# A two-layer transformer on one core: in the first feed-forward, half of the row transposes go from the matrix engine to VectorE and DMA, and the order of the weight chunks changes

## The chip, the cores and the metric

The kernel runs on one core of one Trainium2 chip. The metric is the device time of one execution in microseconds (us); runs are compared by their medians. The engines are called by the names that the profile uses: PE is the matrix engine (PEld its weight loads), DVE is VectorE, ACT is ScalarE, POOL is GpSimd, SP is the engine that issues most DMAs.

## The reference, cut to what matters

The input is x with 2 sequences of 512 rows of 512 floats. Four blocks follow one another, each with a residual and a layernorm: a linear attention over a fixed memory, a feed-forward with ternary weights, a softmax attention, and an ordinary gated feed-forward. The change touches the second block and the end of the first:

```python
def _L0_ffn_ref(x, w_gate, w_up, w_down):
    xf = x.astype(jnp.float32) / 128.0
    gate = jnp.einsum('bsh,ih->bsi', xf, w_gate)
    up = jnp.einsum('bsh,ih->bsi', xf, w_up)
    inter = jax.nn.silu(gate) * up
    inter_q = jnp.trunc(jnp.clip(inter * 128.0, -128.0, 127.0)).astype(jnp.int8)
    down = jnp.einsum('bsi,hi->bsh', inter_q.astype(jnp.float32), w_down)
    out = jnp.trunc(jnp.clip(down * 128.0, -128.0, 127.0)).astype(jnp.int8)
    return out
...
x = _layernorm(x + _L0_attn_ref(x, ...), axis=-1)
x = _layernorm(x + _L0_ffn_ref(x, w_gate, w_up, w_down), axis=-1)
```

The intermediate size is 1376, which the kernel cuts into 11 chunks: ten of 128 and a last one of 96.

## The kernel before, in words

Rows lie 128 to a tile, so each sequence has four row tiles `xs[b][0..3]`. A matmul needs the rows transposed, with the 512 features on the partitions in four blocks of 128.

**The end of the first attention.** `read` (L392) takes one row tile: eight PE products, one per head (L401), four heads at a time. For each head ACT reads the denominator (L405); DVE takes the reciprocals (L409); ACT scales the first three heads (L414) and POOL adds them (L418, L427), and DVE adds the other five to the row (L423). The loop at L516 reads the eight row tiles in order, and inside tile i it normalizes tile i-1: `norm_a0` (L495) takes the statistics on DVE, the reciprocal root on POOL (L143, L144), the offset on DVE (L503), and writes the normalized row on ACT (L504).

**The transposed rows of the first feed-forward.** `split(b)` (L254) makes them for one sequence. For each block k, PE transposes the four row tiles into one PSUM bank (L264), ACT copies the bank to SBUF rounded to the short format [...] (`his`, L265), and DVE keeps the rest (`los`, L266). Sequence 0 is turned in the loop at L516, while the tiles 5 and 6 are read; sequence 1 is turned in the feed-forward, between its third and fourth chunk (L678 to L681).

**The chunks.** `up(b, c)` (L560) multiplies chunk c of the gate weights, then of the up weights, with the rows of sequence b: 16 matmuls of 128x512 into two PSUM banks (L567). There are eight banks in all, so PE can be about four chunks ahead of those who empty them. A chunk is finished by a chain that changes engine at nearly each step:

- ACT: silu of the gate, `sg` (L583)
- DVE: times the up half, `y` (L586), then cut to 12 bits (L155)
- ACT: two relus that round toward zero, `ta` and `tb` (L165, L166)
- DVE: their difference is the integer row, `it` (L593)

The weights themselves are divided by their scale on ACT (`divided`, L506, done in L433), into tiles `tu` of which four fit (`query_tile`, L278); chunks 0 to 2 are divided in the loop at L516 by the text, chunks 3 to 10 in the feed-forward, a half after each chunk (L597). `largest` (L172) reads the first tile of the down weights on DVE (L177); PE, DVE and POOL make of it the scale (L184, L195, L199) and the 11 divided tiles `td` (L435), which DVE compares with the originals (`check_down`, L204).

**What sets the order.** Each engine runs its own list in order. For PE, ACT, DVE and SP a scheduler makes the lists at build time from the program's text, the dependences and the `issue_after` ties; POOL keeps the order of the text. So where a helper is called in the text is not always where its instructions stand. In the built program of before, the divisions of chunks 0 to 3 stand on ACT ahead of the eight reads. By chunk the text has (0,0) to (0,2), the transposes of sequence 1, (0,3), (1,0) to (1,2), then the two sequences by turns, (0,4), (1,3), (0,5), (1,4) and so on. The down products follow at L617 and L710 to L725. SP issues the eleven loads of the down weights (L248) when the attention's buffers are free.

Of the kernel before, what the change touches and what calls it, by code (L numbers as in the profile page):

```python
# [10 lines left out]
F32 = mybir.dt.float32  # L11
F32R = mybir.dt.float32r
I32, I16, I8 = mybir.dt.int32, mybir.dt.int16, mybir.dt.int8
PE = mybir.EngineType.PE
AF = mybir.ActivationFunctionType
ALU = mybir.AluOpType
# [3 lines left out]
P = 128  # L20
B, S, HID = 2, 512, 512
NT = S // P
NK = HID // P
NH, G, D = 8, 4, 128
INTER = 1376
CHUNKS = [(i, min(P, INTER - i)) for i in range(0, INTER, P)]
GROUPS = [4, 4, 3]
LN_EPS = 1e-5
DEN_EPS = 1e-6
LAST = HID - 1  # L30
LENT = 3
TOP12 = -4096
BELOW_HALF = 0.5 - 2.0**-13
# [3 lines left out]
def kernel(  # L37
# [19 lines left out]
    nc = tc.nc  # L57
# [6 lines left out]
    xtp = ctx.enter_context(tc.tile_pool(name="xtp", bufs=2))  # L64
# [14 lines left out]
    def psum(name):  # L79
        return ps.tile([P, 512], F32, tag="mm", name=name)  # L80
# [99 lines left out]
    def over_partitions(mx, name):  # L180

        k = mx.shape[-1]
        pm = psum(f"pmx_{name}")
        nc.tensor.transpose(pm[:k, :P], mx, ident)  # L184
        top = small.tile([k, 1], F32, tag=f"top{k}", name=f"top_{name}", bufs=1)
        nc.vector.reduce_max(top, pm[:k, :P], AX.X)
        dg = small.tile([k, k], F32, tag=f"dg{k}", name=f"dg_{name}", bufs=1)
        nc.vector.tensor_scalar_mul(dg, ident[:k, :k], top)
        return dg

    def scales(dg, name):

        k = dg.shape[-1]
        pb = psum(f"pbc_{name}")
        nc.tensor.matmul(pb[:, :k], ones[:k, :], dg, start=True, stop=True)  # L195
        sc = const.tile([P, k], F32, tag=f"sc_{name}", name=f"sc_{name}")
        nc.vector.tensor_scalar(sc, pb[:, :k], 1e-30, 3e38, ALU.max, ALU.min)
        inv = const.tile([P, k], F32, tag=f"inv_{name}", name=f"inv_{name}")
        nc.vector.reciprocal(inv, sc)  # L199
        return sc, inv  # L200
# [50 lines left out]
            wds.append(wd)  # L251
        return wds

    def split(b):  # L254

        hi = xtp.tile([P, NK, S], F32, tag="xt", name=f"xh_{b}").bitcast(F32R)
        los = [pair_tile(f"xl_{b}_{i}").bitcast(F32R) for i in range(2)]
        his = [hi[:, k, :] for k in range(NK)]
        los = [los[k // 2][:, k % 2, :] for k in range(NK)]

        def block(k):
            pt = psum(f"pt_f0{b}_{k}")
            for t in range(NT):
                nc.tensor.transpose(pt[:, ts(t, P)], xs[b][t][:, ts(k, P)], ident)  # L264
            nc.scalar.copy(his[k], pt)  # L265
            nc.vector.tensor_sub(los[k], pt, his[k].bitcast(F32))  # L266

        return his + los, block


    wop = ctx.enter_context(tc.tile_pool(name="wop", bufs=6))
# [6 lines left out]
    def query_tile(name):  # L278
        return wqp.tile([P, 2, HID], F32, tag="wq", name=name)

    with tc.tile_pool(name="a0w", bufs=1) as a0w, tc.tile_pool(name="a0", bufs=2) as a0:
# [213 lines left out]
        def norm_a0(i, steps):  # L495

            b, t = order[i]
            with tc.issue_after(steps[1].ins):
                stats = layernorm_stats(xs[b][t], f"a0{b}_{t}")
            with tc.issue_after(steps[-1].ins):  # L500
                mv, rstd = stats
                off = small.tile([P, 1], F32, tag="off", name=f"off_{i}")
                nc.vector.tensor_scalar(off, mv[:, 0:1], rstd, -1.0, ALU.mult, ALU.mult)  # L503
            nc.scalar.activation(xs[b][t], xs[b][t], AF.Identity, bias=off, scale=rstd)  # L504

        def divided(c, a):  # L506
            n = CHUNKS[c][1]
            if c not in ts_up:
                t = query_tile(f"tu_{c}").bitcast(F32R)
                ts_up[c] = t.rearrange("p a (k i) -> p a k i", k=NK)  # L510
                if n < P:
                    nc.gpsimd.memset(ts_up[c][:, :, :, n:].bitcast(F32), 0.0)
            ternary(nc.scalar, ts_up[c][:, a, :, :n], gus[c][:, a], inv_up[:, a : a + 1])

        ts_up, x2 = {}, []
        for i, (b, t) in enumerate(order):  # L516
            steps = read(b, t, lambda steps: norm_a0(i - 1, steps) if i else None)
            for _ in range((3, 2, 2, 0, 0, 0, 0, 0)[i]):
                check_up(*checks.pop(0))
            if i == 3:  # L520
                tot_up = total(counts, "up")
            elif i == 4:
                flag_up, eff_up = verdict(tot_up, sc_up, "up")
            if i in (3, 4, 5):
                for a in range(2):
                    divided(i - 3, a)
            if i == 5:
                parts, block = split(0)
                x2.append(parts)
            if i in (5, 6):  # L530
                for k in range(2):
                    block(2 * (i - 5) + k)
        norm_a0(len(order) - 1, steps)


    fp = ctx.enter_context(tc.tile_pool(name="fp", bufs=2))

    def inter_tiles(name, dtype=F32):
# [6 lines left out]
            for b in range(B)  # L545
        ]

    wdp = ctx.enter_context(tc.tile_pool(name="wdp", bufs=1))
    wds = down_weights(wd0_in, "0")
    with tc.tile_pool(name="f0", bufs=2) as f0:  # L550
# [9 lines left out]
        def up(b, c, behind=()):  # L560
            n = CHUNKS[c][1]
            t = ts_up[c]
            pp = [psum(f"pg_f0{b}_{c}"), psum(f"pu_f0{b}_{c}")]
            with tc.If(ternary_up > 0) as way:
                for a in range(2):
                    for i in range(2 * NK):
                        nc.tensor.matmul(  # L567
                            pp[a], t[:, a, i % NK, :], x2[b][i],
                            start=(i == 0), stop=(i == 2 * NK - 1),
                        )  # L570
            with way.Else():
                for a in range(2):
                    for i in range(2 * NK):
                        nc.tensor.matmul(
                            pp[a][:n], gus[c][:, a, i % NK, :],
                            x2[b][i].bitcast(F32),
                            start=(i == 0), stop=(i == 2 * NK - 1),
                        )
            sg = fp.tile([P, S], F32, tag="sg", name=f"sg_f0{b}_{c}")
            with ExitStack() as tied:  # L580
                for step in behind:
                    tied.enter_context(tc.issue_after(step.ins))
                nc.scalar.activation(sg[:n], pp[0][:n], AF.Silu, scale=silu_scale[:n])  # L583
            y = f0.tile([P, S], F32, tag="y", name=f"y_f0{b}_{c}")

            step = nc.vector.scalar_tensor_tensor(  # L586
                y[:n], sg[:n], eff_up[:n, 1:2], pp[1][:n], ALU.mult, ALU.mult
            )
            cut_to_12(y[:n])
            ta, tb = truncated_parts(f0, y[:n], n, f"f0{b}_{c}")  # L590

            it = its[b][c // 4][:, c % 4]
            nc.vector.scalar_tensor_tensor(  # L593
                it[:n], tb[:n], 128.0, ta[:n], ALU.min, ALU.subtract
            )
            inter[b].append(it)
            if to_divide:  # L597
                part = to_divide.pop(0)
                if part:
                    divided(*part)  # L600
            return step

        to_divide = [(c, a) for c in range(3, len(CHUNKS)) for a in range(2)]

        counts_d = const.tile([P, len(CHUNKS)], F32, tag="counts_d", name="counts_d")
        nc.gpsimd.memset(counts_d, 0.0)
# [25 lines left out]
            return pd  # L632


        pds, ys, stats, moved = {}, {}, {}, {}

        def scaled(i):
            y = f0.tile([P, HID], F32, tag="y", name=f"yd_{i}")
            moved[i] = nc.scalar.activation(y, pds[i], AF.Copy, scale=down_scale)
            cut_to_12(y)  # L640
            ys[i] = y

# [29 lines left out]
            with tc.issue_after(taken[n if t == NT - 1 else f"f0_{n}"].ins):  # L672
                layernorm_apply(xs[b][t], xs[b][t], stats[i])

        to_divide[2:2] = [None, None]
        for c in range(3):
            up(0, c)
        parts, block = split(1)  # L678
        x2.append(parts)
        for k in range(NK):  # L680
            block(k)  # L681
        step = up(0, 3)
        with tc.issue_after(step.ins):
            mx_d = largest([wds[0]], "down")
        for c in range(3):
            up(1, c)
        top_d = over_partitions(mx_d, "down")
        for c in range(4, 8):
            up(0, c)
            if c == 4:  # L690
                sc_d, inv_d = scales(top_d, "down")
            up(1, c - 1)
            for i in range(2 * c - 8, 2 * c - 6):
                check_down(i)
        up(0, 8)
        up(1, 7)
        check_down(8)
        check_down(9)
        up(0, 9)
        check_down(10)  # L700
        up(0, 10)
        tot_d = total(counts_d, "down")
        up(1, 8)
        flag_d, eff_d = verdict(tot_d, sc_d, "down")
        down_scale = const.tile([P, 1], F32, tag="down_scale", name="down_scale")
        nc.vector.tensor_scalar(down_scale, eff_d, -128.0, None, ALU.mult)
        up(1, 9)
        ternary_d = branch(flag_d)
        for i in range(2):
            f0_down(i)  # L710

        up(1, 10, moved.values())
        for i in range(2, len(order) - 2):
            f0_down(i)

# [565 lines left out]
```

## Time and profile before

| What | us |
|---|---|
| median of the runs (lowest, highest; 3 runs) | 472.47 (472.12, 472.58) |
| the profiled execution: its own time | 471.99 |
| the profiled execution: its span, first to last instruction | 470.0 |
| last read of the attention: PE's last product issued | 130.2 |
| first chunk of the feed-forward: PE's first matmul | 130.65 |
| transposes of sequence 1 on PE | 141.99 to 147.58 |
| end of the first feed-forward on PE | 234.1 |

The times in the last four lines count from the span's start. The chain of waits is followed back from the last instruction: each line has start, length, engine and operation. The timeline has start, length, engine, line, operation, output and inputs, and in square brackets how long the engine had been idle and who ended that. The matmuls of PE are pipelined: a record of 128x512 lasts 0.39 us, and the next one starts 0.23 us after it did.

### The profile page before, as it was taken

To read this page: it belongs to the slowest core of one execution; us is meant where nothing else is said; L and a number is where in the kernel's file an instruction comes from. 1 tells how busy PE (TensorE), PEld (TensorE's weight loads), DVE (VectorE), ACT (ScalarE), POOL (GpSimd) and SP (SyncE) were. 2 spreads that over 40 slices of the span, in tenths; PEclk is the share of its full clock that TensorE was granted. 3 is DMA by queue.
4 is the path that set the end of the run, shared out by engine and by line. 5 is a ranking of instruction groups with operands and counts; after the bars stand their busy time and mean duration, and the time that the engine had idled before them with its cause. 6 is when DMAs were issued, how large, how long until landed. Compare 5 with 4: busy or idle time off the path is not lost.

```text
span 470.0 us, 5725 instructions
## 1 busy us (share of the span) xinstructions
PE 463.0 (99%) x1899; PEld 330.7 (70%) x1899; DVE 327.9 (70%) x622; ACT 268.1 (57%) x507; POOL 114.4 (24%) x141
## 2 busy tenths in 40 slices
PE   9999999999999999999999999999999999999995
PEld 8454444434478788888866568888888888888885
DVE  1265677767857677755988989986666767998633
ACT  3344799557556877645756743575644768532201
POOL 0343101566460090400348032000000000041101
PEclk9999999999999999999999999999999999999998
DMA  8999800000015000213192000000000000001011
GB/s 311 373 348 382 301 2 0 0 0 3 1 54 188 3 1 1 92 47 81 58 360 94 0 1 1 1 0 1 1 0 1 0 1 1 1 24 45 22 46 45
DMA packets 15187, 33.97 MB, mean 72 GB/s; under 512 B 3440, under 2 KB 4336, under 8 KB 15152
## 3 DMA queue, kind: packets, MB, share of 16 engines
q1 hardware_dynamic: 14864, 33.14, 19.6%
q8 instruction: 22, 0.36, 0.3%
q10 hardware_dynamic: 288, 0.36, 0.2%
q14 instruction: 13, 0.11, 0.1%
HBM read 31.40 MB, written 2.10 MB: 71 GB/s over the span
## 4 chain that ended last, share of the span: by engine, by line
PE 72%; ACT 7%; DVE 5%; issue 3%; POOL 0%; POOLq 0%; DVEq 0%; ACTq 0%
PE pm L1071 17%; PE pg_f L567 9%; PE pu_f L567 8%; PE pc L1071 8%; PE pdm L1159 7%; PE pd_f L622 4%; PE pdc L1159 4%; DVE x L423 4%; PE pqk L853 3%; PE po L401 2%; ACT y L414 2%; ACT t L433 2%; PE pv L866 2%; PE pot L949 1%; PE po L965 1%
## 5 line engine op out<-in xcount | busy, mean ns | idle before, releaser
L401 PE MATMUL po<-mw,q 128*128 128x512 f32 x128 | 57.1, 598 | 0.3 <-DVE mv_a L137 0.2
L325 PE MATMUL pq<-xt_a,wq 128*128 128x512 f32 (+1 forms) x152 | 56.9, 526 | 0.0
L143 POOL TENSOR_TENSOR rstd_f<-mv_f,ln_eps 128x1 f32<-128x1 f32 x15 | 4.4, 295 | 172.1 <-DVE mv_f L1174 130.2
L401 PEld LDWEIGHTS po<-mw,q 128*128 128x128 f32 x128 | 23.0, 189 | 32.1 <-issue 17.7
L325 PEld LDWEIGHTS pq<-xt_a,wq 128*128 128x128 f32 x152 | 26.2, 190 | 27.3 <-issue 26.2
L1071 PE MATMUL pm<-r,ugu 128*128 128x512 f32 x152 | 37.7, 389 | 0.0
L1071 PE MATMUL pm<-r,it_early 128*128 128x512 f32 x144 | 36.7, 392 | 0.0
L1071 PEld LDWEIGHTS pm<-r,ugu 128*128 128x128 f32 x152 | 28.5, 188 | 5.9
L1071 PEld LDWEIGHTS pm<-r,it_early 128*128 128x128 f32 x144 | 27.0, 188 | 6.0 <-issue 0.5
L423 DVE SCALAR_TENSOR_TENSOR x<-po,den,x 128x511 f32<-128x511 f32 x40 | 29.8, 745 | 1.9
L165 ACT ACTIVATE ta_f<-y_f,below_half 128x512 int8<-128x512 f32 (+1 forms) x22 | 15.9, 723 | 23.7 <-DVE y_f L155 23.3
L1081 DVE SCALAR_TENSOR_TENSOR ev_q<-pm,ev_q 128x512 f32<-128x512 f32 x27 | 18.6, 687 | 14.1 <-PE pm L1071 14.1
L418 POOL TENSOR_TENSOR y<-y,y 128x511 f32<-128x511 f32 x16 | 20.3, 1272 | 31.5 <-ACT y L414 30.8
L593 DVE SCALAR_TENSOR_TENSOR it_f<-tb_f,ta_f 128x512 fp32r<-128x512 int16 (+1 forms) x22 | 15.2, 690 | 16.3 <-ACT tb_f L166 16.3
L361 ACT ACTIVATE e<-pq,bq 128x512 f32<-128x512 f32 x16 | 11.1, 691 | 24.1 <-PE pq L325 21.7
L567 PE MATMUL pg_f<-xh,tu 128*128 128x512 f32 x88 | 24.7, 401 | 0.0
L1080 ACT ACTIVATE ev_q<-pc 128x512 f32<-128x512 f32 x27 | 16.0, 594 | 14.1 <-PE pc L1071 14.0
L435 POOL TENSOR_SCALAR td<-wd,inv_down 128x512 fp32r<-128x512 f32 x11 | 18.6, 1710 | 22.0 <-DVE inv_down L199 22.0
L567 PE MATMUL pg_f<-xl,tu 128*128 128x512 f32 x88 | 23.6, 390 | 0.0
L567 PE MATMUL pu_f<-xh,tu 128*128 128x512 f32 x88 | 23.6, 389 | 0.0
L567 PE MATMUL pu_f<-xl,tu 128*128 128x512 f32 x88 | 23.5, 389 | 0.0
L961 ACT ACTIVATE x<-x,off_f,rstd_f 128x512 f32<-128x512 f32 x7 | 5.7, 816 | 27.7 <-POOL off_f L960 27.7
(310 smaller groups left out, 1088.3 us busy)
## 6 DMA issues: line engine op xcount, KB each, us to landing
gu<-in_gu SPq DMA_DIRECT2D x20, 512.0 KB, 8.0
wo<-in_wo SPq DMA_DIRECT2D x16, 512.0 KB, 5.7
wd<-in_wd SPq DMA_DIRECT2D x20, 256.0 KB, 4.9
wq<-in_wq SPq DMA_DIRECT2D x8, 256.0 KB, 4.1
x<-in_x SPq DMA_DIRECT2D x7, 256.0 KB, 4.4
out<-x SPq DMA_DIRECT2D x7, 256.0 KB, 2.0
wqkv<-in_wqkv SPq DMA_DIRECT2D x1, 768.0 KB, 10.7
m<-in_m SPq DMA_DIRECT2D x1, 512.0 KB, 5.8
```

The source lines that it names most:

```text
L165: nc.scalar.activation(a[:n], y, AF.Relu, bias=below_half[:n])
L325: done = nc.tensor.matmul(pq[:, at], wq[h][:, k, :], xt[:, k, at], start=(k == 0), stop=(k == NK - 1),)
L401: nc.tensor.matmul(po, qs[b][h0 + j][:, ts(t, P)], mw[:, h0 + j, :], start=True, stop=True,)
L418: nc.gpsimd.tensor_add(ys[0][:, :LAST], ys[0][:, :LAST], y[:, :LAST])
L423: steps.append(nc.vector.scalar_tensor_tensor(x[:, :LAST], four[j][:, :LAST], d, x[:, :LAST], ALU.mult, ALU.add))
L435: eng.tensor_scalar(out, w, factor, None, ALU.mult)
L567: nc.tensor.matmul(pp[a], t[:, a, i % NK, :], x2[b][i], start=(i == 0), stop=(i == 2 * NK - 1),)
L622: nc.tensor.matmul(pd, inter[b][c][:, ts(t, P)], td[c].bitcast(F32R), start=(c == 0), stop=(c == last),)
L1071: nc.tensor.matmul(p, w, x, start=(left[id(p)] == begun[id(p)]), stop=(left[id(p)] == 1))
L1080: nc.scalar.activation(ev, pc, AF.Copy, scale=CROSS)
L1081: nc.vector.scalar_tensor_tensor(ev, pm, MAIN, ev, ALU.mult, ALU.add)
L1159: nc.tensor.matmul(p[:, :w], got[j // 4][1][kind][:, j % 4], down_parts[j][kind][:, cols], start=(j == 0 and kind == kinds[0]), stop=(j == ...
```

## The change

Sequence 0 is still transposed on PE. For sequence 1, DVE transposes each normalized row tile in squares of 32x32 into a tile `squares` (one instruction of 128x512 per row tile), and then 16 DMAs on SP put the squares where a full transpose has them: each moves 32 partitions by 16 runs of 32 floats. `block` reads the result from SBUF.

```diff
+SQ = 32
+LEAD = 6
...
-    def split(b):
+    def split(b, xt=None):
...
         def block(k):
-            pt = psum(f"pt_f0{b}_{k}")
-            for t in range(NT):
-                nc.tensor.transpose(pt[:, ts(t, P)], xs[b][t][:, ts(k, P)], ident)
-            nc.scalar.copy(his[k], pt)
-            nc.vector.tensor_sub(los[k], pt, his[k].bitcast(F32))
+            h, l = his[k], los[k]
+            if xt is None:
+                rows = psum(f"pt_f0{b}_{k}")
+                for t in range(NT):
+                    nc.tensor.transpose(rows[:, ts(t, P)], xs[b][t][:, ts(k, P)], ident)
+            else:
+                rows = xt[:, :, k, :]
+                h, l = (u.rearrange("p (t q) -> p t q", t=NT) for u in (h, l))
+            return (
+                nc.scalar.copy(h, rows),
+                nc.vector.tensor_sub(l, rows, h.bitcast(F32)),
+            )
...
+    def move_squares(squares, xt):
+        src = squares.rearrange("p t (k i) -> p (t k) i", k=NK)
+        dst = xt.rearrange("p t k i -> p (t k) i")
+        for i in range(P // SQ):
+            for j in range(P // SQ):
+                nc.sync.dma_start(dst[ts(j, SQ), :, ts(i, SQ)], src[ts(i, SQ), :, ts(j, SQ)])
...
-                t = query_tile(f"tu_{c}").bitcast(F32R)
+                t = (pair_tile if c in PAIRED else query_tile)(f"tu_{c}").bitcast(F32R)
...
+        PAIRED = (LEAD - 2, LEAD - 1, len(CHUNKS) - 1)
+        def turn_squares(i):
+            b, t = order[i]
+            nc.vector.transpose(squares[:, t, :], xs[b][t])
...
-            if i in (3, 4, 5):
+            if i >= len(order) - LEAD:
                 for a in range(2):
-                    divided(i - 3, a)
+                    divided(i - len(order) + LEAD, a)
...
+            if i > NT:
+                turn_squares(i - 1)
         norm_a0(len(order) - 1, steps)
+        turn_squares(len(order) - 1)
...
+    xt1 = fp.tile([P, NT, NK, P], F32, tag="it11", name="xt_f01", bufs=1)
+    move_squares(squares, xt1)
...
-            if to_divide:
-                part = to_divide.pop(0)
-                if part:
-                    divided(*part)
+            for part in to_divide.get((b, c), ()):
+                divided(*part)
...
+        to_divide = {
+            (1, c - LEAD): [(c, a) for a in range(2)] for c in range(LEAD, len(CHUNKS))
+        }
...
-        for c in range(3):
-            up(0, c)
-        parts, block = split(1)
+        for c in range(LEAD - 1):
+            step = up(0, c)
+        parts, block = split(1, xt1)
         x2.append(parts)
-        for k in range(NK):
-            block(k)
-        step = up(0, 3)
+        moved = [ins for k in range(NK) for ins in block(k)]
+        up(0, LEAD - 1, moved)
         with tc.issue_after(step.ins):
             mx_d = largest([wds[0]], "down")
-        for c in range(3):
-            up(1, c)
+        up(1, 0)
+        up(1, 1)
         top_d = over_partitions(mx_d, "down")
-        for c in range(4, 8):
+        last = len(CHUNKS) - 1
+        for c in range(LEAD, last + 1):
             up(0, c)
-            if c == 4:
+            if c == LEAD:
                 sc_d, inv_d = scales(top_d, "down")
-            up(1, c - 1)
-            for i in range(2 * c - 8, 2 * c - 6):
+            up(1, c - LEAD + 2)
+            for i in range(2 * (c - LEAD), 2 * (c - LEAD) + 2):
                 check_down(i)
...
```

By chunk the order is now (0,0) to (0,5), (1,0), (1,1), then (0,6), (1,2), (0,7), (1,3) and so on to (0,10), (1,6), then (1,7) to (1,10), with the down products of sequence 0 around the last of them as before. `up` also ties `y`, not only `sg`, behind the steps that it is given, so in chunk (0,5) both stand behind the four copies and four subtractions of `block`. Chunks 0 to 5 are divided before the feed-forward, chunk c from 6 on after (1, c-6). In the built program this moves two divisions, of the chunks 4 and 5, from the feed-forward into the reads of the tiles 6 and 7.

On each engine's list of the built program, the pieces stand as follows. DVE: the squares of the tiles 4 and 5 (the first two of sequence 1) inside the reads of the tiles 6 and 7, the squares of tile 6 between the statistics of the last row tile and their sum, the squares of tile 7 between `y` and the cut of chunk (0,0). SP: the first five loads of the down weights, the 16 moves, the other six loads. ACT: `ta` and `tb` of chunk (0,4), the four copies of `block`, then `sg` of (0,5). DVE there: `y` of (0,4), `largest`, the cut and `it` of (0,4), the four subtractions.

More of the change, by code (lines that the diff above doesn't have):

```diff
@@ L529 @@
                 x2.append(parts)
+                squares = xtp.tile([P, NT, HID], F32, tag="xt", name="squares")
             if i in (5, 6):
@@ L583, in up @@
                 nc.scalar.activation(sg[:n], pp[0][:n], AF.Silu, scale=silu_scale[:n])
[L584 to L588, printed above, removed]
+                y = f0.tile([P, S], F32, tag="y", name=f"y_f0{b}_{c}")
+                step = nc.vector.scalar_tensor_tensor(
+                    y[:n], sg[:n], eff_up[:n, 1:2], pp[1][:n], ALU.mult, ALU.mult
+                )
             cut_to_12(y[:n])
@@ L596, in up @@
             inter[b].append(it)
-            if to_divide:
-                part = to_divide.pop(0)
-                if part:
-                    divided(*part)
-            return step
-        to_divide = [(c, a) for c in range(3, len(CHUNKS)) for a in range(2)]
+            for part in to_divide.get((b, c), ()):
+                divided(*part)
+            return step
+        to_divide = {
+            (1, c - LEAD): [(c, a) for a in range(2)] for c in range(LEAD, len(CHUNKS))
+        }
         counts_d = const.tile([P, len(CHUNKS)], F32, tag="counts_d", name="counts_d")
@@ L632, in down @@
             return pd
-        pds, ys, stats, moved = {}, {}, {}, {}
+        pds, ys, stats, scaling = {}, {}, {}, {}
         def scaled(i):
             y = f0.tile([P, HID], F32, tag="y", name=f"yd_{i}")
-            moved[i] = nc.scalar.activation(y, pds[i], AF.Copy, scale=down_scale)
+            scaling[i] = nc.scalar.activation(y, pds[i], AF.Copy, scale=down_scale)
             cut_to_12(y)
@@ L673, in normed @@
                 layernorm_apply(xs[b][t], xs[b][t], stats[i])
-        to_divide[2:2] = [None, None]
-        for c in range(3):
-            up(0, c)
-        parts, block = split(1)
+        for c in range(LEAD - 1):
+            step = up(0, c)
+        parts, block = split(1, xt1)
         x2.append(parts)
-        for k in range(NK):
-            block(k)
-        step = up(0, 3)
+        moved = [ins for k in range(NK) for ins in block(k)]
+        up(0, LEAD - 1, moved)
         with tc.issue_after(step.ins):
             mx_d = largest([wds[0]], "down")
-        for c in range(3):
-            up(1, c)
-        top_d = over_partitions(mx_d, "down")
-        for c in range(4, 8):
-            up(0, c)
-            if c == 4:
-                sc_d, inv_d = scales(top_d, "down")
-            up(1, c - 1)
-            for i in range(2 * c - 8, 2 * c - 6):
[L694 to L701, printed above, removed]
+        up(1, 0)
+        up(1, 1)
+        top_d = over_partitions(mx_d, "down")
+        last = len(CHUNKS) - 1
+        for c in range(LEAD, last + 1):
+            up(0, c)
+            if c == LEAD:
+                sc_d, inv_d = scales(top_d, "down")
+            up(1, c - LEAD + 2)
+            for i in range(2 * (c - LEAD), 2 * (c - LEAD) + 2):
+                check_down(i)
+        check_down(last)
+        for c in range(last - LEAD + 3, last - 1):
+            up(1, c)
         tot_d = total(counts_d, "down")
-        up(1, 8)
         flag_d, eff_d = verdict(tot_d, sc_d, "down")
@@ L706 @@
         nc.vector.tensor_scalar(down_scale, eff_d, -128.0, None, ALU.mult)
-        up(1, 9)
+        up(1, last - 1)
         ternary_d = branch(flag_d)
@@ L710 @@
             f0_down(i)
-        up(1, 10, moved.values())
+        up(1, last, scaling.values())
         for i in range(2, len(order) - 2):
```

## The prediction

> **What bounds the kernel now.** I read the page's parts 1 and 4, then the chain in order of time around the change, then the timelines of ACT and DVE over the same stretch, last the DMA rows.
>
> ```profile
> PE 463.0 (99%) x1899; PEld 330.7 (70%) x1899; DVE 327.9 (70%) x622; ACT 268.1 (57%) x507; POOL 114.4 (24%) x141
> PE 72%; ACT 7%; DVE 5%; issue 3%; POOL 0%; POOLq 0%; DVEq 0%; ACTq 0%
> ```
>
> PE is busy nearly always and the chain is mostly PE: what PE no longer does is saved, and what PE waits for is lost, unless a later wait absorbs it. The chain at the place of the change (start, length, what):
>
> ```profile
> 140.33 1.82 PE pu_f L567 x8
> 142.15 1.42 PE pt_f L264 x13
> 143.57 1.85 PE pg_f L567 x8
> 145.43 1.82 PE pu_f L567 x8
> 147.25 0.33 PE pt_f L264 x3
> 147.58 2.10 PE pg_f L567 x8
> 149.68 1.82 PE pu_f L567 x8
> 151.50 1.81 PE pg_f L567 x8
> ```
>
> A chunk on PE is 1.82 + 1.81 = 3.63 us. From 142.15 to 151.50 there are two chunks, (0,3) and (1,0): 9.35 us for 7.26. The transposes of sequence 1 and the waits around them thus cost 2.09 us. This is all that the change can win on PE.
>
> The timeline of ACT (start, length, engine, line, what, idle before) shows how far the finishing of chunks lags:
>
> ```profile
> 139.80 0.82 ACT L504 ACTIVATE x<-x,off,rstd_a 128x512 f32<-128x512 f32 x1 [0.53 <-DVE off L503]
> ...
> 141.35 0.72 ACT L165 ACTIVATE ta_f<-y_f,below_half 128x512 int8<-128x512 f32 x1 [0.15 <-DVE y_f L155]
> ...
> 143.82 0.67 ACT L583 ACTIVATE sg_f<-pg_f,silu_scale 128x512 f32<-128x512 f32 x1
> ...
> 149.33 0.68 ACT L583 ACTIVATE sg_f<-pg_f,silu_scale 128x512 f32<-128x512 f32 x1
> 151.84 0.72 ACT L165 ACTIVATE ta_f<-y_f,below_half 128x512 int8<-128x512 f32 x1 [1.83 <-DVE y_f L155]
> ...
> 163.01 0.67 ACT L583 ACTIVATE sg_f<-pg_f,silu_scale 128x512 f32<-128x512 f32 x1
> 165.05 0.72 ACT L165 ACTIVATE ta_f<-y_f,below_half 128x512 int8<-128x512 f32 x1 [1.36 <-DVE y_f L155]
> 165.68 0.71 ACT L166 ACTIVATE tb_f<-y_f,below_half 128x512 int16<-128x512 f32 x1
> 166.29 0.67 ACT L583 ACTIVATE sg_f<-pg_f,silu_scale 128x512 f32<-128x512 f32 x1
> ```
>
> Each silu follows the second relu of the chunk before it, and that relu hangs on y and the cut on DVE. So ACT and DVE walk one chain, and a chunk takes 166.29 - 163.01 = 3.28 us however idle they look: hardly faster than PE. The silu of (0,2) starts at 143.82, though PE began that chunk at 138.35 (timeline of PE); the lag comes from the end of the attention, and PE bridges it with its PSUM banks.
>
> [...] No row of this trace has a DVE transpose. [...] DVE rows of 128x512 in the trace take 0.43 (L155) to 0.74 us (L586). [...] PE's last matmul starts at 464.13, and the granted clock (the column before the last two) falls.
>
> ```profile
> 463.00:467.00 4.00, 1.41 (x12) 1.21 (x11) 1.93 (x5) 0.46 (x1) 0.84 (x1) 0.95 0.00 0
> 467.00:470.00 3.00, 0.00 (x0) 0.00 (x0) 0.00 (x0) 0.00 (x0) 0.00 (x0) 0.50 0.26 87
> ```
>
> **Removed:** 16 transposes and their waits, -2.09 us.
>
> **The squares, d each.** Bounds 0.43 (the quickest row) and 1.36 (two passes of 0.68); I take d = 0.65. The first two fall into gaps of DVE in the reads of tiles 6 and 7: after the third-head step, at 122.1 and 130.2, DVE waits 2.1 us for ACT's denominators. Nothing. The third stands between the statistics (L135, 137.70) and their sum (L137), so the sum, POOL's root, the offset and the normalization of the last row come d later: 139.80 + d. The fourth waits for that row, and the cut of (0,0) and all DVE work are queued behind it. The row ends at 140.62 + d, the square at 140.65 + 2d = 141.95, the cut, 0.43, at 142.38, and the first relu starts at 142.4 instead of 141.35: 1.07 later. This lag passes on; PE doesn't feel it yet.
>
> **ACT gets to sequence 1's copies late.** These four copies stand behind both relus of (0,4). The silu of (0,2) moves from 143.82 to 144.89. The lag of before between 143.82 and 149.33 came from the copies that stood there and is gone, so two loops of 3.28 lead to the silu of (0,4) at 151.45. In that chunk `largest` stands between y and the cut, as it did after the silu at 149.33: 151.84 - 149.33 = 2.51 to the relu, so 153.96. The second relu follows 0.63 later, the first copy 0.61 after that: 155.20. Copies from SBUF to SBUF take 0.62 (L763); the fourth ends at 157.68.
>
> **What PE does meanwhile.** It runs six chunks without a gap, since the banks of (0,0) to (0,2) are free in time (y of (0,2) ends near 146.4; (1,0) wants that bank at 152.9). It would start (1,0) at 138.35 + 4 x 3.63 = 152.87 and its fourth matmul, which needs the fourth copy, at 153.55. The copy comes at 157.70: a wait of 4.15 us. The subtractions, 0.68 each behind the copies, end about 158.5 and are wanted from 157.93 to 158.6: nothing more.
>
> **The 16 moves** issue from 141.95, behind five loads of 0.52 us each from 137.7. The nearest row loads 512 pieces of 128 bytes, just one move's size:
>
> ```profile
> L740 SPq DMA_DIRECT2D gu<-in_gu x1: 508/508/508, 219.6 to 219.6; - x1
> ...
> DMA to landing us min/median/max: 3.9/3.9/3.9
> ```
>
> At 0.51 us of issue the last starts at 149.6 and lands at 153.5. The copies want it at 155.2: hidden by 1.7 us. If the DMA engines set the pace: L740 and its follower kept them busy from 221.6 to 223.2, 0.8 us each. First work comes 1.0 us after the issue (219.2 to 220.2), landing 0.5 after the last: 141.95 + 1.5 + 16 x 0.8 = 156.3, late by 1.1. At 1.0 us each it is 4.3 late. Even is at 0.73. [...] the issue rate holds; I take that.
>
> **Moved, at no cost, with the cover.** Divisions of chunks 4 and 5, 4 x 0.71 on ACT, go into the reads, where ACT waits 0.6 to 1.05 between denominators; without that cover up to 0.7 per read. Chunk 6 is now divided after (1,0), for use after (1,1): its tile is free when PE leaves (1,0), about 160.7, ACT writes it by 163.1, PE wants it at 164.4. The six down-weight loads behind the moves land by about 160; POOL wants the sixth after 170. POOL's clearing of chunk 10's last columns now waits for (1,4) and holds back seven divisions of 1.7 us: they end near 199, while their sum is wanted after (1,8), near 208. Loads of the next layer start some 8 us later, and ACT reads the first at 248.
>
> **Sum.** 471.99 - 2.09 + 4.15 = 474.05 for the profiled execution. The median of the runs is 0.48 above it: 474.53.
>
> **Rivals.**
> - *The clock falls in the gap.* PE would idle from 153.1 to 155.8, 2.7 us, then run at half load to 157.7. [...] For: at the end of the trace 0.95 over 4 us means 0.4 us at half, so the clock fell at 466.6, 2.2 us after PE's last work. [...] 476.2.
> - *The moves are the bound*, at 0.8 to 1.0 us each: 475.6 to 478.8. For: the last two loads of small pieces; against: they came from HBM.
> - *The lag is gone (not slower).* Were ACT and DVE abreast of PE at (0,4), because without sequence 1's copies the relus overlap with the next chunk, the relus would end as late in the tail: y starts when PE ends, second relu 2.6 us later (192.24 to 194.85), plus 0.6 for `largest`: 149.24 + 3.2 = 152.4. The fourth copy would end at 154.9, a wait of 1.35, and the sum is 471.7. It decides at a first copy before 153.1, where the wait equals the gain. For: ACT has less to do there. Against: the loops of 3.28 in the trace hold with and without divisions in them.
> - *Half of the change does nothing*: if the wait were on PE's side only through the order of chunks, not the squares, the time is the forecast's less 2d: 473.2. It is inside the range and has no case of its own.
>
> **Chances.** 0.2% is 0.94 us, about what a measurement can tell. Forecast 0.42; clock 0.20; moves 0.14; lag gone in part or whole 0.24, of which 0.15 lie within 0.94 us of before, 0.07 are faster and 0.02 slower. Faster 0.07, same 0.15, slower 0.42 + 0.20 + 0.14 + 0.02 = 0.78. With d at its bounds the forecast is 474.1 to 475.9. The range reaches down to 471.5, leaving out about 0.06, and up to 478.5, leaving out the slowest moves, 0.07.
>
> **What would show it.** Right: PE's chunk (1,0) starts about 3 us after (0,5) ends, with ACT's copy as the releaser; DVE transposes near 0.65; silu of (0,4) near 151.5; the last move lands before 155. Wrong: a wait of PE that a DMA ends (moves), a granted clock under 1.00 after 155 (clock), or copies that start before 153.1 (lag gone). If PE's chunks before (0,5) have gaps, the banks or the reads of the attention are the cause, and I have priced neither.

## The result, and the profile after

| | before | after |
|---|---|---|
| median of the runs, us | 472.35 (472.12 to 472.58, 4 runs) | 476.67 (475.64 to 477.10, 4 runs) |
| ratio, 95% interval | | 1.0088 (1.0071 to 1.0106) |
| profiled execution: own time, span | 471.99, 470.0 | 477.1, 475.1 |
| PE's first chunk begins | 130.65 | 131.45 |
| from there to the end of the span | 339.35 | 343.65 |

The change costs 4.3 us; 474.5 had been forecast. The profiled execution is the longest of the four. It loses 0.80 of its 5.1 us before the change begins: near 38 us DVE waits longer for loads of the attention's weights (10.5 us against 8.1 from 20 to 45 us), and PE for DVE (0.51 us against none). The order of work there is the same in both programs, and the start of PE's first chunk scatters from 130.07 to 131.97 over the profiles below. So every trace is counted here from PE's first chunk on, and there the difference is 343.65 - 339.35 = 4.30, the same as between the medians.

The first part of the page and the engines' shares of the chain of waits:

```profile
PE 464.3 (98%) x1883; PEld 330.6 (70%) x1883; DVE 328.9 (69%) x626; ACT 268.3 (56%) x507; POOL 113.4 (24%) x141
PE 66%; ACT 8%; DVE 6%; issue 4%; SPq 2%; POOL 1%; DMA 0%; POOLq 0%; DVEq 0%; ACTq 0%
```

PE has 16 instructions less and is busy 1.3 us longer: part of its work ran slower. SP's queue is new in the chain. PE's timeline around chunk (1,0) (start, length, ..., idle before and who ended it):

```profile
152.75 1.07 PE L598 MATMUL pu_f<-xl,tu 128*128 128x512 f32 x4
157.22 2.35 PE L598 MATMUL pg_f<-xh,tu 128*128 128x512 f32 x4 [3.41 <-ACT xh L274]
159.38 1.91 PE L598 MATMUL pg_f<-xl,tu 128*128 128x512 f32 x4
161.08 1.85 PE L598 MATMUL pu_f<-xh,tu 128*128 128x512 f32 x4
162.77 1.09 PE L598 MATMUL pu_f<-xl,tu 128*128 128x512 f32 x4
163.70 1.09 PE L598 MATMUL pg_f<-xh,tu 128*128 128x512 f32 x4
```

The first chunk takes 4.07 us in all these traces and five more take 3.63 each, so (1,0) is due 22.20 us after the first began, at 153.65. It starts at 157.22, 3.57 late, when ACT's copy `xh` comes. Then groups of four matmuls take 2.35, 1.91 and 1.85 us where 1.07 is usual, and the chunk lasts until 163.70: 6.48 us for 3.63, another 2.85. The table by windows shows why (window, length, then PE's busy time and instructions; the column before the last two is the granted clock):

```profile
153.00:155.00 2.00, 0.82 (x4) 0.35 (x2) 1.37 (x3) 0.53 (x1) 0.00 (x0) 1.00 0.59 98
155.00:156.00 1.00, 0.00 (x0) 0.00 (x0) 0.17 (x1) 0.80 (x2) 0.00 (x0) 0.95 0.72 123
156.00:159.00 3.00, 1.78 (x4) 1.08 (x5) 2.32 (x4) 2.45 (x5) 0.00 (x0) 0.50 0.90 250
159.00:162.00 3.00, 3.00 (x9) 2.32 (x9) 1.79 (x4) 1.40 (x3) 0.00 (x0) 0.50 0.72 261
162.00:163.00 1.00, 1.00 (x4) 0.79 (x3) 0.69 (x1) 0.82 (x2) 0.00 (x0) 0.64 0.00 0
```

A mean of 0.95 over the second stretch means 0.1 us at half clock: the clock falls at 155.9, 2.1 us after PE's last work ended (152.75 + 1.07). By the last row it is back at 162.7. The account: -2.09 for the transposes, +3.57 wait, +2.85 clock, together 4.33 (measured 4.30).

Why the copy is late, in ACT's timeline:

```profile
151.97 0.67 ACT L614 ACTIVATE sg_f<-pg_f,silu_scale 128x512 f32<-128x512 f32 x1
154.47 0.72 ACT L167 ACTIVATE ta_f<-y_f,below_half 128x512 int8<-128x512 f32 x1 [1.83 <-DVE y_f L157]
155.09 0.70 ACT L168 ACTIVATE tb_f<-y_f,below_half 128x512 int16<-128x512 f32 x1
156.55 2.18 ACT L274 CAST xh<-xt_f 128x512 fp32r<-128x512 f32 x4 [0.76 <-DMA xt_f<-squares]
```

The second relu of (0,4) ends at 155.79, 2.1 us after PE wanted (1,0). Then ACT waits 0.76 more for the last move. So two things are late together, ACT's place on its own list and the moves. The rows of the moves (ns min/median/max of issuing one, first and last start; then from issue to landing):

```profile
L287 SPq DMA_DIRECT2D xt_f<-squares x16: 591/627/1832, 142.6 to 154.4; - x16
DMA to landing us min/median/max: 2.1/2.1/4.0
```

### The profile page after: what moved, and what is told of

It is laid out like the page before. It is cut to its first block, busy times and chain, and to the rows that moved or that the text cites. A ratio compares the mean times of both kernels' runs of the same rounds, so it can differ in the third digit from the quotient of the medians.

```text
span 475.1 us, 5717 instructions
## 1 busy us (share of the span) xinstructions
PE 464.3 (98%) x1883; PEld 330.6 (70%) x1883; DVE 328.9 (69%) x626; ACT 268.3 (56%) x507; POOL 113.4 (24%) x141
## 4 chain that ended last, share of the span: by engine, by line
PE 66%; ACT 8%; DVE 6%; issue 4%; SPq 2%; POOL 1%; DMA 0%; POOLq 0%; DVEq 0%; ACTq 0%
PE pm L1096 17%; PE pc L1096 8%; PE pdm L1184 7%; PE pg_f L598 7%; PE pu_f L598 6%; DVE x L442 4%; PE pd_f L653 4%; PE pdc L1184 4%; PE pqk L878 3%; ACT y L433 2%; SPq L287 2%; ACT t L452 2%; PE pv L891 2%; PE pot L974 1%; PE po L990 1%
## 5 line engine op out<-in xcount | busy, mean ns | idle before, releaser
L420 PEld LDWEIGHTS po<-mw,q 128*128 128x128 f32 x128 | 23.0, 189 | 32.2 <-issue 17.8
L598 PEld LDWEIGHTS pg_f<-xh,tu 128*128 128x128 f32 x88 | 16.7, 192 | 8.2 <-ACT xh L274 4.5
```

The lines of the kernel that those rows point to most:

```text
L420: nc.tensor.matmul(po, qs[b][h0 + j][:, ts(t, P)], mw[:, h0 + j, :], start=True, stop=True,)
L598: nc.tensor.matmul(pp[a], t[:, a, i % NK, :], x2[b][i], start=(i == 0), stop=(i == 2 * NK - 1),)
```

## The experiments

The theory from this profile: PE waits because ACT, which finishes chunks behind PE, reaches the copies late; the moves end barely later; and the gap then also costs the clock. The rivals: only the moves are late; the clock is a side matter; the new order, the squares or the moved divisions cost something themselves. The table gives, for every kernel, how late (1,0) starts, what it takes beyond 3.63, and the sum of both with the 2.09 us gained, beside what the trace shows from PE's first chunk to the end against the 339.35 of before. (For e1, which keeps the transposes, nothing is gained, and the 2.1 us that they take there are not counted as late; for e2 the 1.81 of added work is in the sum.) The last column is the ratio of the runs to those of before on the same chip.

| kernel | late | slower | sum | trace | median, us | ratio (95%) |
|---|---|---|---|---|---|---|
| the change | 3.57 | 2.85 | +4.33 | +4.30 | 476.67 | 1.0088 (1.0071 to 1.0106) |
| e1 order alone | 0 | 0 | 0 | -0.02 | 471.67 | 0.9999 (0.9990 to 1.0008) |
| e2 more work in the gap | 1.47 | 1.08 | +2.27 | +2.18 | 475.01 | 1.0060 (1.0046 to 1.0075) |
| e3 ready data, copies late | 2.71 | 3.20 | +3.82 | +3.75 | 474.58 | 1.0053 (1.0040 to 1.0066) |
| e4 ready data, copies early | 0 | 0 | -2.09 | -2.20 | 470.15 | 0.9964 (0.9951 to 0.9977) |
| e5 seven ahead, copies later too | 2.38 | 2.08 | +2.37 | +2.28 | 474.61 | 1.0053 (1.0039 to 1.0066) |
| e6 seven ahead, copies in place | 0.98 | 1.09 | -0.02 | -0.06 | 471.61 | 0.9999 (0.9984 to 1.0014) |
| e7 copies early | 3.05 | 2.17 | +3.13 | +3.06 | 475.60 | 1.0078 (1.0064 to 1.0093) |
| e8 copies early, two queues | 0.01 | 0.34 | -1.74 | -1.69 | 470.40 | 0.9969 (0.9957 to 0.9980) |
| e9 as e3, no squares | 1.90 | 2.59 | +2.40 | +2.29 | 474.42 | 1.0045 (1.0032 to 1.0058) |
| e10 two queues, copies late | 2.74 | 2.01 | +2.66 | +2.61 | 474.79 | 1.0063 (1.0040 to 1.0087) |

The sums meet the traces within 0.11 us everywhere. From PE's first chunk on, what happens at this one chunk is thus the whole of the difference, to within 0.11 us.

**e1, the order alone.** The squares and the moves are taken out, and sequence 1 is transposed on PE again, between (0,4) and (0,5).

```diff
-            if i > NT:
-                turn_squares(i - 1)
...
-        turn_squares(len(order) - 1)
...
-    move_squares(squares, xt1)
...
-        parts, block = split(1, xt1)
+        parts, block = split(1)
```

> The new order of chunks and the new places of the divisions alone: no squares, no moves, sequence 1 transposed on PE between (0,4) and (0,5). Theory (PE waits for late copies, and then runs at half clock): PE gets its 2.09 us of transposes back and loses the wait; the copies, behind the silu of (0,4), end near 154.2 and (1,0) is due near 155.0, so no wait: 472.4, within 0.4. Rival 'the order or the moved divisions cost something themselves' (the attention's reads, which I did not price): 473.2 or more, with PE's first chunk later than in the kernel before. Rival 'the six chunks ahead help by themselves': under 471.9.

Measured 471.67, ratio 0.9999: no difference. Six chunks ahead, the divisions in the reads and POOL's later clearing cost nothing and bring nothing, within 0.1% or 0.5 us.

**e2, more work in the gap.** The gate half of (0,5) is computed twice.

```diff
-        def up(b, c, behind=()):
+        def up(b, c, behind=(), times=1):
...
-                for a in range(2):
+                for a in [0] * times + [1]:
...
-        up(0, LEAD - 1, moved)
+        up(0, LEAD - 1, moved, times=2)
```

> The changed kernel with work added: the gate half of (0,5), eight matmuls, is computed twice into the same bank (1.82 us more of PE, same result). Clock theory: PE now idles 3.57 - 1.82 = 1.75 us instead of 3.6; in the changed kernel the granted clock fell 2.1 us after PE's last work, so now it does not fall, and the 2.85 us that chunk (1,0) ran longer come back: 476.67 - 2.85 = 473.8, faster though it does more. Rival 'the clock is a side matter, the wait is all': the added work lies in the wait, 476.7. Rival 'PE is the bound there': 478.5.

PE's timeline, and then the window after the gap with its clock:

```profile
155.08 1.07 PE L598 MATMUL pu_f<-xl,tu 128*128 128x512 f32 x4
157.45 2.07 PE L598 MATMUL pg_f<-xh,tu 128*128 128x512 f32 x4 [1.30 <-ACT xh L274]
159.35 1.12 PE L598 MATMUL pg_f<-xl,tu 128*128 128x512 f32 x4
```

```profile
156.00:159.00 3.00, 1.65 (x4) 0.56 (x3) 2.26 (x4) 2.54 (x6) 0.00 (x0) 1.00 0.92 253
```

PE idles 1.30 us and the clock holds at 1.00 (the mean clock of all six runs is 0.997 or 0.998, against 0.991 to 0.994 in the changed kernel). With eight matmuls more, the kernel is 2.1 us shorter by its trace and 1.3 by the ratios (1.0060 to 1.0088). Of the 2.1 us, 0.3 come from moves that ended earlier here: the first copy starts 24.81 us after PE's first chunk instead of 25.10. The other 1.8 are the clock, so it is no side matter. It is less than the 2.85 expected, because the first four matmuls still take 2.07: they come at the pace of ACT's copies, one every 0.5 us, which the half clock had covered in the changed kernel. That pace costs 1.08.

**e3, ready data, copies late.** The moves are left out. The copies read the row tiles as they are, not transposed, tied behind the same relu.

```diff
...
+        tbs.append(nc.scalar.activation(b[:n], y, AF.Relu, bias=below_half[:n], scale=-1.0))
...
-                rows = xt[:, :, k, :]
-                h, l = (u.rearrange("p (t q) -> p t q", t=NT) for u in (h, l))
+                rows = xt[k]
...
-    move_squares(squares, xt1)
+    xt1 = xs[1]
...
-        moved = [ins for k in range(NK) for ins in block(k)]
+        with tc.issue_after(tbs[-1].ins):
+            moved = [ins for k in range(NK) for ins in block(k)]
```

> The squares are made, the 16 moves are left out: the copies of sequence 1 read the row tiles as they are (not transposed, so these rows are wrong), at the same place on ACT's list, behind both relus of (0,4). The data are ready at 142. Lag theory (ACT comes to the copies late, the moves ended only 0.76 us after that): the first copy starts at 155.8 instead of 156.55, PE still waits 2.8 us, and at half clock, so 475.9. Rival 'the moves are the bound': no wait, 476.67 - 3.57 - 2.85 = 470.25. Rival 'the shorter gap saves the clock': 473.

**e4, ready data, copies early.** The same without the tie.

> As the run with ready data, but the copies stand where the scheduler puts them, ahead of the relus of (0,2). (Moves left out, rows of sequence 1 not transposed.) Lag theory: with data and place both early PE does not wait at (1,0), 470.2 (the gain of 2.09 us alone). Rival 'the four copies and subtractions then push the lag of ACT and DVE by 2.5 us and PE waits for banks instead': 471 to 473. Rival 'something outside this place costs': over 474.

The copy in ACT's timeline of e3, which waits for nothing, and what PE did:

```profile
155.46 2.17 ACT L275 CAST xh<-x 128x512 fp32r<-128x512 f32 x4
```

```profile
156.11 2.36 PE L598 MATMUL pg_f<-xh,tu 128*128 128x512 f32 x4 [2.53 <-ACT xh L275]
```

Without any move the first copy stands at 155.46, 24.26 us after PE's first chunk; in the changed kernel it was at 25.10. PE still waits 2.53 and loses the clock, for 6.83 us here (155.54 to 162.37). So ready data alone bring 0.55 us of the 6.4 at stake (trace), and e4, where ACT reaches the copies early as well, brings all of it: 470.15, 2.20 us under before by its trace. "Only the moves are late" is refuted. By the medians (474.58, where 475.9 was expected) e3 gained more than its trace says. Its profiled run, 476.39, is the longest of its five and has a mean clock of 0.991; the other four have 0.993 or 0.994, and 0.994 is what the profiled runs of e5, e7 and e10 have, whose traces show half clock for 3.41 us. That these four lost it for 3.41 us and not 6.83 is likely, but no trace of them shows it.

**e5 and e6, seven chunks ahead.** In e5 the copies keep their place relative to (1,0), behind the relus of (0,5); in e6 they stay behind those of (0,4). The divided chunk 6 lies in the tile that takes sequence 1's integer rows of the chunks 8 to 10 later on (`it12`), and POOL clears that tile's last rows only afterwards.

```diff
-LEAD = 6
+LEAD = 7
...
-                    divided(i - len(order) + LEAD, a)
+                    divided(i - 2, a)
...
+    tu6 = fp.tile([P, 3, S], F32, tag="it12", name="tu_6", bufs=1)[:, :2].bitcast(F32R)
...
+        to_divide[0, 1], to_divide[0, 2] = [(6, 0)], [(6, 1)]
...
```

In e6 in addition:

```diff
-        for c in range(LEAD - 1):
+        for c in range(LEAD - 2):
...
-        up(0, LEAD - 1, moved)
+        up(0, LEAD - 2, moved)
+        up(0, LEAD - 1)
```

> Seven chunks of sequence 0 ahead instead of six, with sequence 1's copies at the same relative place on ACT: behind both relus of (0,5), ahead of the silu of (0,6). (The divided weights of chunk 6 lie in a tile that is free until (1,8); ACT divides them after (0,0) and (0,1).) PE has 3.63 us more of work and wants (1,0) 25.8 us after its first chunk began; the moves end at 25.1. Lag theory: ACT comes to the copies one loop of 3.28 us later as well, at 27.6, PE still waits some 2.4 us and may lose the clock: -2.09 + 2.4 + 1 to 2.85 against the kernel before, 473.3 to 475.2. Rival 'only the moves are late': no wait at all, 470.2.

> Seven chunks ahead, but the copies stay where the changed kernel has them on ACT, behind the relus of (0,4) and ahead of the silu of (0,5). They start when the moves end, 25.1 us after PE's first chunk began, and PE wants them from 25.8 on: no idle, at most the pace of the subtractions, 0.5. Lag theory and moves theory alike: -2.09 + 0 to 0.5, 470.2 to 470.7, faster than both kernels. Rival 'the copies then make the relus of (0,5) and (0,6) late and PE waits for banks or results': 472 or more.

ACT's and PE's timelines of e5, then those of e6:

```profile
158.21 2.17 ACT L274 CAST xh<-xt_f 128x512 fp32r<-128x512 f32 x4
```

```profile
158.87 2.36 PE L599 MATMUL pg_f<-xh,tu 128*128 128x512 f32 x4 [2.22 <-ACT xh L274]
```

```profile
156.45 2.18 ACT L274 CAST xh<-xt_f 128x512 fp32r<-128x512 f32 x4 [1.79 <-DMA xt_f<-squares]
```

```profile
157.12 2.06 PE L599 MATMUL pg_f<-xh,tu 128*128 128x512 f32 x4 [0.81 <-ACT xh L274]
```

In e5 the last move had started at 153.3, and the data were there. The copy begins at 158.21, 27.54 after PE's first chunk (27.6 expected), and waits for nothing but ACT's own list. More chunks ahead do not remove the wait if the copies move back with them. The gap is 2.22 us, and the clock still falls, at 159.3. In e6 PE idles 0.81 and the clock holds in the profile, but the time only equals that of before, outside the 470.2 to 470.7 expected: the copies wait for the moves until 26.14 and PE is 0.98 late, and their pace costs 1.09 where I had said 0.5 at most. Three of its 14 runs took 473.8 to 474.1; none of the three was traced.

**e7, copies early with one queue.** The copies stand one chunk earlier on ACT's list, with the moves as they are.

```diff
-        for c in range(LEAD - 1):
-            step = up(0, c)
+        for c in range(LEAD - 2):
+            up(0, c)
...
-        up(0, LEAD - 1, moved)
+        step = up(0, LEAD - 2, moved)
+        up(0, LEAD - 1)
```

> The changed kernel with the copies one chunk earlier on ACT's list, behind the relus of (0,3) and ahead of the silu of (0,4). Theory (the place on ACT and the end of the moves lie within 0.8 us of each other): the copies now wait for the moves until the same 156.55, so PE waits as long, 476.6, and ACT stands idle for it. Rival 'the place is the bound, the moves could have been used earlier': 475.8. Rival 'the relus of (0,4) and (0,5), now 4 us later, hold up PE': 477.5 or more.

```profile
155.47 2.18 ACT L274 CAST xh<-xt_f 128x512 fp32r<-128x512 f32 x4 [3.97 <-DMA xt_f<-squares]
```

Now ACT stands idle for the moves. The start of the copy, 24.58 after PE's first chunk, is 0.52 earlier than in the changed kernel; the slowest issue of a move took 1.31 us here and 1.83 there, so most of this is the moves' own scatter. The median, 475.60, is nearer to the rival's 475.8 than to my 476.6; by the ratios e7 gains 0.5 us on the changed kernel (1.0078 against 1.0088), which is within their intervals. So the times do not decide. What does is the line above, in which ACT stands idle until the last move has landed. The place alone brings little.

**e8 and e10, two queues.** Eight moves on SP's queue and eight on POOL's, which has none to issue in the trace of the change from 136 to 158 us. In e8 the copies also stand early, as in e7; in e10 late, as in the change.

```diff
-                nc.sync.dma_start(dst[ts(j, SQ), :, ts(i, SQ)], src[ts(i, SQ), :, ts(j, SQ)])
+                eng = nc.sync if j % 2 else nc.gpsimd
+                eng.dma_start(dst[ts(j, SQ), :, ts(i, SQ)], src[ts(i, SQ), :, ts(j, SQ)])
```

> The copies early as in the run beside this one, and the 16 moves shared between SP's queue and POOL's, eight each, at the same time. If one queue's issue rate (0.67 us from one move to the next) is what makes the moves late, eight take 5.4 us and the last lands near 150 to 151; the copies start at 152.1, PE gets the first at 152.8 and wants it at 153.65: no wait, 470.2 to 470.7. Rival 'the DMA engines are the limit, two queues only share them': the last lands near 156, 476.6. Rival 'POOL's queue is slow, over 1.2 us a move': 473 to 475.

> The moves on two queues, the copies where the changed kernel has them (behind the relus of (0,4)). The moves land some 4 us earlier than in the changed kernel; by the place theory that is worth only what the run with ready data gained: first copy at 24.3 to 24.4 after PE's first chunk began, PE idles 2.7 us and loses the clock, 474.6. Rival 'the early moves were what made the run with two queues and early copies fast': 470.4.

The moves of e8, ACT's copy and PE's chunk (1,0):

```profile
L288 SPq DMA_DIRECT2D xt_f<-squares x8: 620/794/1827, 141.8 to 148.4; - x8
L288 POOL DMA_DIRECT2D xt_f<-squares x8: 648/650/992, 142.5 to 147.4; - x8
```

```profile
151.28 2.19 ACT L274 CAST xh<-xt_f 128x512 fp32r<-128x512 f32 x4
```

```profile
152.85 1.17 PE L599 MATMUL pg_f<-xh,tu 128*128 128x512 f32 x4
```

The last issue starts 17.8 us after PE's first chunk instead of 22.9, the copies begin as soon as ACT comes to them, and PE starts (1,0) on time. 470.40 is less than either kernel takes: 0.9969 of before (0.9957 to 0.9980); one of its 22 runs took 474.78, at a mean clock of 0.994. e10 has the same moves and loses it all again, 474.79 (474.6 expected):

```profile
154.92 2.17 ACT L274 CAST xh<-xt_f 128x512 fp32r<-128x512 f32 x4
```

```profile
155.58 2.36 PE L599 MATMUL pg_f<-xh,tu 128*128 128x512 f32 x4 [2.56 <-ACT xh L274]
```

Its copies wait for no data and start at 24.28 after PE's first chunk, within 0.02 of e3. Each cure alone leaves the wait; both together remove it.

**e9, as e3 without the squares.**

```diff
-            if i > NT:
-                turn_squares(i - 1)
...
-        turn_squares(len(order) - 1)
```

> The run with ready data and late copies once more, now without the four squares on DVE as well (moves and squares left out, rows of sequence 1 read as they are). If the third and fourth square, 0.69 each and 0.4 less where the cut came sooner, put about 1.1 us into the lag of ACT and DVE as the prediction had it, the first copy comes 1.1 us earlier after PE's first chunk began (23.2 instead of 24.35), PE idles 1.6 instead of 2.7 us; at that length the clock may hold (it held at 1.3 and fell at 2.2): 471.5 to 473.5. Rival 'the squares are hidden, the lag is all ACT's': first copy at 24.35, 474.6 as before.

```profile
155.16 2.06 PE L594 MATMUL pg_f<-xh,tu 128*128 128x512 f32 x4 [1.75 <-ACT xh L275]
```

```profile
156.75:157.00 0.25, 0.25 (x1) 0.25 (x2) 0.25 (x1) 0.25 (x1) 0.00 (x0) 1.00 0.00 0
157.00:157.25 0.25, 0.25 (x2) 0.21 (x2) 0.25 (x2) 0.25 (x1) 0.00 (x0) 0.86 0.00 0
157.25:157.50 0.25, 0.25 (x2) 0.15 (x2) 0.25 (x1) 0.01 (x1) 0.00 (x0) 0.50 0.00 0
```

The first copy comes 23.45 after PE's first chunk instead of 24.26: the squares put 0.81 us into the lag. The forecast of a clock that holds failed for most runs. The profiled one lost it at 157.2, after PE had resumed at 155.16. The 22 runs fall into two groups by mean clock: 7 at 0.997 or 0.998 with a median of 473.1 us, and 15 at 0.994 or 0.995 with 474.6. Of the 29 runs of before beside them, one is below 0.996. In the trace the clock is at half from 157.18 to 160.60; half a clock for 3.41 us is 3.41 x 0.5 / 472 = 0.0036 of mean clock, about this difference. The 1.5 us between the medians fit the trace too: the chunk is 2.59 slower with the clock lost, and the pace of the copies alone cost 1.08 in e2. So the same program, which idles 1.75 us in the trace, seems to keep the clock in some runs and to lose it in most; the gaps of the other runs were not traced.

## Why it came out so, by the prediction's steps

**The gain of 2.09 us: right.** e4 shows 2.20 and e8, with real moves, 1.69.

**The squares: right in size.** 0.69 to 0.71 us each (0.65 taken). Into the lag they put 0.81 and not 1.07: the third delays the last row's normalization by only 0.44 (9.59 against 9.15 us after PE's first chunk).

**ACT late at the copies: right.** The silu of (0,4) was to start 20.8 us after PE's first chunk, and did at 20.5; ACT was to be free for the copies at 24.55, and was at 24.34. The loops of 3.28 are there (145.41, 148.69, 151.97).

**What PE waits: right, with errors that partly cancel.** I had 4.15: 2.7 of idle before the first copy, then half load until the fourth. In the change PE idles 3.41 and (1,0) is 3.57 late; the pace of the copies costs 1.08 more where the clock holds (e2). That makes 4.65. The moves added 0.76 that I had taken to be hidden. The copies follow one another every 0.52 us, not every 0.62, which takes some 0.3 off.

**"At 0.51 us of issue the last starts at 149.6 and lands at 153.5": wrong.** The moves start every 0.67 us, one issue took 1.83, and the last starts 4.0 us later than forecast. It lands 2.1 us after its issue and not 3.9, which gives 1.8 back by luck: 25.05 us after PE's first chunk and not 22.85. "The issue rate holds" was right in that the DMA engines were not the limit (55% busy from 147 to 154). It was my assumption, though: the trace of before has no such move inside SBUF, and the rate of 0.51 us a move came from a load out of HBM (L740, 508 ns). The slower issue cost the change 0.76 us, yet it is why e7 fails and e8 needs two queues.

**"The clock falls in the gap": this is the step that failed.** I left the clock out of the sum and gave the rival 0.20. The clock fell in every profile with a gap of 2.22 to 3.41 us, inside the gap (the change, e3) or at most 0.65 us after its end (e5, e7, e10), and in e9's, with a gap of 1.75, 2.0 us after its end. The sign for it was in my own text: the trace of before has a fall 2.2 us after PE's last work, and I gave it too little weight. I took the 2.7 us of idle that I forecast as too short for a fall, which no trace showed. With the clock held the change would have cost -2.09 + 3.57 + 1.08 = +2.56, near the forecast's +2.06; the other 1.77 us are the clock. The measured 476.67 lies in the range because the range took in this rival, not because the forecast's sum held.

That the rival's 476.2 comes so near is in part luck. It stands 1.7 us above the forecast, an estimate that the trace of before did not show. Half of the 3.41 us that the clock was down in e5 comes to as much, but in the change it was down for 6.83. While PE waits or goes at the pace of the copies, the half clock costs little: from the first group of four matmuls to the next it is 2.16 us in the change and 1.90 in e2. Beyond the pace of 1.08, half clock for 3.41 us cost 0.9 to 1.1 us (e5, e7, e10), or 1.5 where the clock fell after the copies had been made (e9), and for 6.83 us it cost 1.8 (the change) and 2.1 (e3).

**What was priced at nothing: right.** e1, and the sums of all traces, leave at most 0.1 us for the divisions, the later clearing or the weight loads.

## What to carry to other kernels

Work that is moved off the bound engine comes back through whoever hands over the result: look where that step stands on its own engine's list, and how far this engine lags, before asking when the data are ready. When two causes are late together, removing one alone may show little; try both before giving either up. A gap of PE can have two prices, its length and the clock after it: here 1.75 us of idle in e9's trace cost both, and the clock then stayed at half for 3.41 us.

## What was not expected of the hardware

- The half clock outlasted the gap. Read from the mean clock of stretches of 0.25 us, it lasted 3.41 us in e5 (159.33 to 162.74), e7 (156.79 to 160.20), e9 (157.18 to 160.60) and e10 (155.92 to 159.33), each to about 0.01, and twice that, 6.83, in the change (155.90 to 162.73) and in e3 (155.54 to 162.37). In e3 PE was at work again from 156.11, so it ran at half clock for another 6.26 us.
- The fall did not come at a fixed time after PE's last work before the gap: that was 2.1 us in the change, 2.0 in e3, 2.7 in e5, 2.9 in e10, 3.5 in e7 and 3.8 in e9, in the last four with PE at work again. The clock held with 0.81 us of idle (e6) and 1.30 (e2), and fell in the trace of e9 with 1.75. Why it fell when it did, and why it stayed down for 3.41 us in some traces and 6.83 in others, these runs do not show.
- A move of 64 KB inside SBUF in pieces of 128 bytes took 0.63 us to issue on SP's queue and landed 2.1 us after; the load from HBM in pieces of the same size took 0.51 and 3.9. On POOL's queue one took 0.65, and both queues worked at the same time; then a move landed 3.2 us after its issue.
